# Unread products in other PSUM banks, and in more waits, of a twelve-section attention and ffn kernel

## The chip, the cores and the metric

The kernel runs on one core of a Trainium2 chip. The metric is the device time of one execution in microseconds. The median of three runs before the change is 3731.08 us (3728.47 to 3732.46).

## The reference

The state x is 16 sequences of 64 tokens with 256 features (1024 tokens in all, float32). A context of 16 x 1601 x 256 is read by four cross attentions. Twelve sections follow one another, each adding to x what it computes from a layer norm of x:

```python
x = x + L0_xattn(ln(x), ctx, ctx)     # 16 heads, softmax, a mask from tril and zero scores
x = x + L0_attn(ln(x))                # encoder of four layers with linear attention, elu(q)+1, and a relu ffn
x = x + L0_ffn(ln(x))                 # 8 experts with a capacity
x = x + L1_xattn(ln(x), ctx)          # slots: three rounds, a GRU cell
x = x + L1_attn(ln(x))                # softmax attention, 16 heads within a sequence of 64
x = x + L1_ffn(ln(x))                 # 8 small experts, two rounds
x = x + L2_xattn(ln(x), ctx, mask)    # relu squared in place of softmax
x = x + L2_attn(ln(x))                # linear attention over 64 random features per head
x = x + L2_ffn(ln(x))                 # 16 experts and a shared one
x = x + L3_xattn(ln(x), ctx)          # softmax over 1601 keys
x = x + L3_attn(ln(x))                # softmax attention with a position bias and a causal mask
x = x + L3_ffn(ln(x))                 # rows rounded to int8, an integer product
```

Each of these is written out here as a name and a note; the change touches no arithmetic of any of them.

## The kernel before, in words

The 1024 tokens are eight tiles of 128 (a tile holds two sequences), and the 256 features are two chunks of 128. The sections run in the order of `STAGES`; each opens its own pools of SBUF and PSUM tiles and closes them at its end. PSUM has eight banks of 128 x 512 float32, and each section shares them out by tags: `mm` with two or three banks for short products, `acc` for accumulators, and others. A tile of a tag has as many banks as `bufs` says. A new tile of a tag waits until the bank's last tile has been read for the last time.

Tile (the framework) plans the order of instructions from a model of their durations. Where `self.pinned` is true, the tensor engine's products (`mm`, line 2617) and transposes (`tr`, line 2630) are kept in the order in which the program calls them. The plain helpers `transpose` (line 174) and `lin_t` (line 195) call the engine themselves and are never pinned. Every engine works through its own queue in order, and an instruction that waits holds up what is behind it.

**Unread products.** `awake(pool, n, tag, bufs)` (line 2623) takes one PSUM tile of the named tag and has the tensor engine multiply the identity with 512 columns of constants into it, n times. Nobody reads the result. Each such product shows as two matmul records. In the profile they are the tile `awake`. Before the change they are called at these places that the change touches:

- `attend` in `l0_attn` (line 686) is a generator, run in turn with `project` of the other half of the tokens. For layer 0's first half (`early`) two products stand in front of `turn(s, 0)`.
- `l2_attn`: the loop at its end calls two in front of the last `project` (line 2116), in a bank of `mm`.
- `Then.turn` (line 2388), the start of the last ffn for a tile: seven, four and three for tiles 0, 6 and 7, in `mm`.
- `token_attention` (line 2652) is the body of L1 and of L3 attention; `own_input` is true for L1. Its inner `linear` normalises and transposes half of the tokens, then makes queries, keys and values; `scores(t)` and `values(t, e)` follow tile by tile, and `project(t)` two tiles later. In `values`, two groups of four transposes go to banks of `mm`, ScalarE copies them to `eT`, and `acc` (one buffer of two banks) takes the products with the values; VectorE's `rec` and then `hT` (lines 2775 and 2776) read `acc`. Unread products stand in front of the transposes (line 2755) and in front of `acc` (line 2761), and for L3 in front of the first `lin_t` (line 2699), all in `mm` with two banks.

Two more sections come into it. `l0_xattn` computes maxima of the scores per block (`maxima`, line 288), eight products per block into the four banks of the tag `w`, ahead of its main stream; `stream` (line 2504) pins the order from its step -1 on, so the first maxima are not pinned. `l2_xattn` normalises all tiles, transposes them and makes the queries through `acc` (two banks); `bk` (two banks) first serves the stream's projections of the context.

Of the kernel before, what the change touches and what calls it, by code (L numbers as in the profile page):

```python
# [12 lines left out]
F32 = mybir.dt.float32  # L13
# [7 lines left out]
P = 128  # L21
B, S, D = 16, 64, 256
T = B * S
NT = T // P
# [40 lines left out]
class Sections:  # L65
# [157 lines left out]
    def l0_xattn(self):  # L223
# [6 lines left out]
        with ExitStack() as ctx:  # L230
# [57 lines left out]
            def maxima(x, g, i):  # L288


                pm = quad()
                for r in range(4):
                    o = slice(32 * r, 32 * r + 32)
                    self.mm(
                        pm[:, r, :], x.qb[o, g].rearrange("p h s -> p (h s)"), x.kT[i][o, g, :512], start=True, stop=True)
                if i == 0:
                    nc.vector.scalar_tensor_tensor(x.z[:, g], pm[:, :, :S], 0.0, tril, ALU.is_equal, ALU.mult)
                    nc.vector.scalar_tensor_tensor(pm[:, :, :S], x.z[:, g], NEVER, pm[:, :, :S], ALU.mult, ALU.add)
                nc.vector.tensor_reduce(x.m4[:, g, :, i], pm, AX.X, ALU.max)  # L299
# [181 lines left out]
    def l0_attn(self):  # L481
# [25 lines left out]
        with ExitStack() as ctx:  # L507
# [178 lines left out]
            def attend(s, w, early=False):  # L686

                kvs = {}

                def sums(t):  # L690

                    pk = ps_kv.tile([P, 2, 512], F32, tag="kv", name="pk")
                    for g in range(2):
                        for j in range(2):
                            o = slice(j * S, (j + 1) * S)
                            self.mm(
                                pk[:, j, g * 136 : (g + 1) * 136], s.kz[o, t, g * P : (g + 1) * P], s.va[o, t, g, :],
                                start=True, stop=True)
                    kv = sb2.tile([P, 2, 2, 136], F32, tag="kv", name="kv")
                    for j in range(2):  # L700
                        V.tensor_tensor(
                            kv[:, j], pk[:, j, :272].rearrange("p (g x) -> p g x", g=2),
                            mask.unsqueeze(1).to_broadcast([P, 2, 136]), ALU.mult)
                    kvs[t] = kv

                def apply(t):
                    po = ps.tile([P, 2, 136], F32, tag="po", name="po", padded_shape=[P, 2, 256])
                    kv = kvs.pop(t)
                    for g in range(2):
                        for j in range(2):  # L710
                            self.mm(
                                po[j * S : (j + 1) * S, g, :], s.qT[:, g, t * P + j * S : t * P + (j + 1) * S],
                                kv[:, j, g, :], start=True, stop=True)
                    r = sb2.tile([P, 2, 8], F32, tag="r", name="r")
                    V.tensor_scalar(r, po[:, :, 128:136], 1e-6, None, ALU.add)
                    V.reciprocal(r, r)
                    V.tensor_tensor(
                        s.n[:, t, :].rearrange("p (g h e) -> p g h e", g=2, e=16),
                        po[:, :, 0:128].rearrange("p g (h e) -> p g h e", e=16),
                        r.unsqueeze(3).to_broadcast([P, 2, 8, 16]), ALU.mult)  # L720

                for t in range(HT):
                    sums(t)
                    yield
                    if t:
                        apply(t - 1)
                        yield
                apply(HT - 1)
                self.awake(ps, 2 if early else 0, "mm", 3)
                turn(s, 0)  # L730
                yield
                turn(s, 1)
                yield
                for t in range(HT):
                    pm = by_token(w.wo, t, s.hT)
                    V.tensor_tensor(s.y[:, t, :], pm, s.y[:, t, :], ALU.add)
                    if t % 2:
                        measure(s, s.y, t // 2)
                    yield
                    if t % 2:  # L740
                        norm(s, s.y, t // 2)
                        yield
# [1134 lines left out]
    def l2_xattn(self):  # L1877
        nc, tc, d = self.nc, self.tc, self.d
        with ExitStack() as ctx:
# [9 lines left out]
            qT = sb.tile([P, KC, T], F32, tag="qT", name="qT")  # L1889
            for t in range(NT):  # L1890
                self.normed(t, xln[:, t, :])
            self.transpose(ps, xln, xT, tag="acc")
            self.lin_t(ps, wq, xT, lambda n, h, pm: nc.vector.tensor_scalar(
                qT[:, n, h * 512 : (h + 1) * 512], pm, 0.25, None, ALU.mult), tag="acc")
            hT = xT
            own = self.c("own2")
            ones = self.c("ones")[:, :32]
# [49 lines left out]
    def l2_attn(self):  # L1947
        nc, tc, d = self.nc, self.tc, self.d
        F, HT = 64, NT // 2
        with ExitStack() as ctx:  # L1950
# [152 lines left out]
            for t in range(NT + 2):  # L2103
                if t < NT:
                    self.awake(ps, 0 if t else 2, "mm", 2)
                    kp = key_features(t)
                if 0 < t <= NT:
                    apply(t - 1, kvs.pop(t - 1))
                for _ in range((3, 3, 2, 2)[t] if t < 4 else 0):
                    next(rest)  # L2110
                if t == 3:
                    next(rest, None)
                if t < NT:
                    kvs[t] = sums(t, kp)
                if t > 1:
                    self.awake(ps, 2 if t > NT else 0, "mm", 2)
                    project(t - 2)
            self.pinned = False

# [218 lines left out]
    def l3_ffn(self, sb, sb2, ps):  # L2338
# [14 lines left out]
        class Then:  # L2353
# [32 lines left out]
                    xs[t] = sc[:, j : j + 1]  # L2386

            def turn(s, t):
                self.awake(ps, {0: 7, 6: 4, 7: 3}.get(t, 0), "mm", 2)
                pt = ps.tile([P, KC, P], BF16, tag="mm", name="trb", bufs=2, padded_shape=[P, KC, 512])  # L2390
                for c in range(KC):
                    self.tr(pt[:, c, :], xq[t][:, c * P : (c + 1) * P], identb)
                xq[t] = sb2.tile([P, KC, P], BF16, tag="f_qT", name="f_qT")
                nc.scalar.copy(xq[t], pt)
# [228 lines left out]
    def awake(self, pool, n, tag, bufs=None):  # L2623

        if n:
            pm = pool.tile([P, 512], F32, tag=tag, name="awake", **({"bufs": bufs} if bufs else {}))
            for _ in range(n):
                self.mm(pm, self.ident, self.cst[:, :512], start=True, stop=True)

# [22 lines left out]
    def token_attention(self, sb, sb2, ps, w, wo, bias_t, rows, scale, own_input, bias=None, then=None):  # L2652
# [21 lines left out]
        def linear(i):  # L2674
# [21 lines left out]
            nc.gpsimd.tensor_tensor(x, x, bo.unsqueeze(1).to_broadcast([P, HT, D]), ALU.add)  # L2696
            for n in range(4):
                if n == i == 0:
                    self.awake(ps, 0 if own_input else 3, "mm", 2)
                pm = ps.tile([P, 512], F32, tag="mm", name="lin_t", bufs=2)  # L2700
                for k in range(KC):
                    self.mm(pm, w[:, k, n * P : (n + 1) * P], xT[:, k, :], start=(k == 0), stop=(k == KC - 1))
# [48 lines left out]
        def values(t, e):  # L2751


            eT = sb2.tile([P, KC, 4, P], F32, tag="eT", name="eT")
            self.awake(ps, ({1: 2, 2: 1} if own_input else {2: 1}).get(t, 0), "mm", 2)
            for g in range(KC):
                pt = ps.tile([P, 4, P], F32, tag="mm", name="turn", bufs=2)
                for r in range(4):
                    self.tr(pt[:, r, :], e[:, r, 2 * g : 2 * g + 2, :].rearrange("p j s -> p (j s)"), self.ident)
                nc.scalar.copy(eT[:, g], pt)  # L2760
            self.awake(ps, 0 if own_input else {1: 1, 2: 1, 5: 2}.get(t, 0), "mm", 2)
            acc = ps.tile([P, 2, 512], F32, tag="acc", name="acc", bufs=1)
            at = acc[:, :, :256].rearrange("p j (k g s) -> p j k g s", k=2, g=2)
            for k in range(2):
# [12 lines left out]
                hT[:, :, t * P : (t + 1) * P].rearrange("p g (j s) -> p j g s", j=2), at[:, :, 0], rec, ALU.mult)  # L2777

        def project(t):
            pm = ps.tile([P, D], F32, tag="mm", name="lin", bufs=2, padded_shape=[P, 512])  # L2780
            for k in range(KC):
                self.mm(pm, hT[:, k, t * P : (t + 1) * P], wo[:, k, :], start=(k == 0), stop=(k == KC - 1))
# [217 lines left out]
```

## Time and profile before

| | us |
|---|---|
| median of three runs | 3731.08 |
| lowest, highest | 3728.47, 3732.46 |
| the profiled execution | 3730.16 |
| its span, first to last instruction | 3728.4 |
| TensorE matmuls busy | 3499.4 (94%) |
| VectorE, ScalarE, GpSimd busy | 1970.9, 1461.2, 1286.4 |
| mean granted TensorE clock | 0.979 |
| unread products in the profile | 104 with the constants, 5 at the start |

The profile's span is one execution; 1.8 us lie around it. The row PEclk of the page gives, in forty equal slices, the TensorE clock that was granted, in tenths. A timeline line gives the start, the length, the engine, the line of the program, the tile written and those read, and, in brackets, how long the engine had stood idle and which instruction ended that. L2619 and L2631 are the helpers `mm` and `tr`, so tile names tell the products apart. L59 is the helper that pins VectorE, ScalarE and GpSimd in `l0_attn`.

### The profile page before, as it was taken

The numbers are of one execution on the slowest core, as the hardware profiler recorded it, in microseconds if no ns is written. First come the engines' busy times: TensorE is split into PE (matmuls) and PEld (weight loads), VectorE is DVE, ScalarE is ACT, GpSimd is POOL, SyncE is SP. The second block draws the span as 40 slices with busy tenths as digits, with TensorE's granted clock in tenths as the row PEclk, the third lists the DMA queues.
The fourth block names the chain that finished last, engine by engine and source line by source line (L and its number), as shares of the span: only waits on it lengthen the run. The fifth ranks groups of instructions, "written<-read, shape, count | busy, mean of one in ns | idle before, by whom it ended". The sixth has DMA issues, their size and how long they took to land.

```text
span 3728.4 us, 71203 instructions
## 1 busy us (share of the span) xinstructions
PE 3499.4 (94%) x31177; PEld 2200.2 (59%) x31192; DVE 1970.9 (53%) x3645; ACT 1461.2 (39%) x2093; POOL 1286.4 (35%) x784
## 2 busy tenths in 40 slices
PE   9999999998999979999988989999999889999997
PEld 4555555564665655555555666667767655555554
DVE  5344333436555635655656555577767765333445
ACT  2333333333444413444433443466666612111123
POOL 2555555552101113433422100577777630000002
PEclk9999999999999979999999999999999989999998
DMA  4111001101333345442101001211111004111550
GB/s 146 38 38 38 28 30 38 38 8 50 101 93 97 116 133 170 147 147 85 64 26 41 1 6 41 72 57 38 57 38 38 11 2 175 36 41 33 241 214 13
DMA packets 108071, 259.77 MB, mean 70 GB/s; under 512 B 9609, under 2 KB 76172, under 8 KB 105456
## 3 DMA queue, kind: packets, MB, share of 16 engines
q1 hardware_dynamic: 99040, 223.14, 16.8%
q10 hardware_dynamic: 6912, 27.27, 2.3%
q0 software_dynamic: 1808, 4.80, 0.5%
q8 instruction: 245, 4.01, 0.4%
q14 instruction: 66, 0.54, 0.0%
HBM read 248.85 MB, written 6.33 MB: 68 GB/s over the span
## 4 chain that ended last, share of the span: by engine, by line
PE 75%; DVE 13%; ACT 7%; issue 2%; DMA 1%; POOL 0%; SPq 0%; ACTq 0%; DVEq 0%; POOLq 0%
PE sc L2619 15%; PE pk L2619 15%; PE lin L2619 6%; PE acc L2619 6%; PE lin_t L2619 5%; ACT e L358 5%; PE pu L2619 4%; PE gate L2166 3%; PE up L2166 3%; PE lin L216 3%; PE pc L1786 3%; PE prz L2619 2%; PE gelu_t L1700 2%; PE turn L2631 1%; PE pa L2619 1%
## 5 line engine op out<-in xcount | busy, mean ns | idle before, releaser
L2548 POOL TENSOR_TENSOR tot<-tot,e 128x1024 f32<-128x1024 f32 (+1 forms) x340 | 803.2, 2362 | 373.3 <-ACT e L358 251.0
L299 DVE TENSOR_REDUCE m<-sc 128x4 f32<-128x2048 f32 x96 | 220.1, 2293 | 271.3 <-PE sc L2619 270.2
L1929 DVE SCALAR_TENSOR_TENSOR e<-sc,row_L_xattn_nbias,free 128x2048 f32<-128x2048 f32 x104 | 244.3, 2349 | 115.5 <-PE sc L2619 113.1
L1931 ACT ACTIVATE e<-e 128x2048 f32<-128x2048 f32 x104 | 198.7, 1911 | 245.8 <-DVE e L1929 245.8
L358 ACT ACTIVATE e<-sc 128x2048 f32<-128x2048 f32 x104 | 195.2, 1877 | 237.3 <-PE sc L2619 235.7
L2619 PE MATMUL sc<-qb,kT 32*128 32x128 f32 x6656 | 245.0, 283 | 36.2 <-DVE m L313 12.3
L2619 PEld LDWEIGHTS sc<-qb,kT 32*128 32x128 f32 x6656 | 206.1, 187 | 80.6 <-issue 22.4
L2619 PEld LDWEIGHTS acc<-e,v 128*32 128x32 f32 x6656 | 169.7, 109 | 105.3 <-issue 96.0
L2619 PE MATMUL acc<-e,v 128*32 128x128 f32 x6656 | 225.9, 276 | 4.7 <-ACT e L1932 4.7
L2619 PE MATMUL pk<-wv,cT 128*128 128x256 f32 x832 | 209.8, 394 | 0.0
L2619 PE MATMUL pk<-cT,wk 128*128 128x512 f32 (+1 forms) x512 | 206.2, 531 | 3.6 <-DVE rows L329 3.6
L1932 ACT ACTIVATE e<-e 128x2048 f32<-128x2048 f32 x104 | 198.7, 1911 | 3.2
L2619 PE MATMUL pk<-wkv,cT 128*128 128x256 f32 x832 | 196.3, 386 | 0.0
L2619 PE MATMUL pk<-cT,wkv 128*128 128x512 f32 (+1 forms) x512 | 194.9, 522 | 0.0
L2619 PEld LDWEIGHTS pk<-wv,cT 128*128 128x128 f32 x832 | 149.5, 190 | 76.4 <-issue 58.9
L2619 PEld LDWEIGHTS pk<-wkv,cT 128*128 128x128 f32 x832 | 153.2, 190 | 28.5 <-issue 4.3
L1786 PE MATMUL pc<-ew,eh 128*128 128x256 f32 x640 | 156.1, 386 | 0.0
L2170 ACT ACTIVATE g<-gate 128x512 f32<-128x512 f32 x68 | 40.6, 597 | 293.4 <-PE gate L2166 293.4
L2619 PE MATMUL sc<-kT,qb 32*128 32x512 f32 (+2 forms) x1536 | 138.9, 461 | 13.8 <-DVE m L299 2.3
L1319 POOL TENSOR_TENSOR e<-e,mx 128x512 f32<-128x512 f32 x96 | 81.9, 885 | 194.3 <-DVE mx L1318 194.3
L2619 PE MATMUL pu<-cn,e 128*64 128x257 f32 (+1 forms) x1248 | 141.6, 381 | 3.3 <-DMA cn<-in_ctx_n 1.8
L2171 DVE TENSOR_TENSOR hT<-up,g 128x512 f32<-128x512 f32 x68 | 47.0, 691 | 183.2 <-PE up L2166 183.2
(544 smaller groups left out, 6425.2 us busy)
## 6 DMA issues: line engine op xcount, KB each, us to landing
cT<-in_ctx_t SPq DMA_DIRECT2D x128, 832.0 KB, 6.4
cn<-in_ctx_n SPq DMA_DIRECT2D x32, 1664.0 KB, 11.9
piece<-in_ctx_n ACTq DMA_DIRECT2D x32, 640.0 KB, 3.9
w<-in_L_attn_W SPq DMA_DIRECT2D x8, 1024.0 KB, 7.0
piece<-in_ctx_n ACTq DMA_DIRECT2D x16, 384.0 KB, 3.7
w<-in_L_ffn_W SPq DMA_DIRECT2D x16, 256.0 KB, 3.1
down<-in_L_ffn_w_down SPq DMA_DIRECT2D x16, 256.0 KB, 2.8
gate<-in_L_ffn_w_gate SPq DMA_DIRECT2D x16, 256.0 KB, 2.7
```

The costliest lines, as they stand in the source:

```text
L216: nc.tensor.matmul(pm, xT[:, k, t * P : (t + 1) * P], w[:, k, :], start=(k == 0), stop=(k == kc - 1))
L299: nc.vector.tensor_reduce(x.m4[:, g, :, i], pm, AX.X, ALU.max)
L358: nc.scalar.activation(e, pm, AF.Exp, scale=0.25)
L1319: pin(nc.gpsimd.tensor_tensor(p.e, p.e, p.mx.unsqueeze(2).to_broadcast(p.shape), ALU.subtract))
L1700: nc.tensor.matmul(pm, w[:, c, lo : lo + m], cT[:, c, :], start=(c == 0), stop=(c == nk - 1))
L1786: nc.tensor.matmul(pc[:, n, j, :], s.eh[i][:, c, tok], ew2[:, c, cols], start=False, stop=(c == 3))
L1929: nc.vector.scalar_tensor_tensor(e16, pm16, nb, free[:, at : at + P].unsqueeze(1).to_broadcast([P, 16, P]), ALU.add, ALU.mult)
L1931: nc.scalar.activation(e, e, AF.Relu)
L1932: nc.scalar.activation(e, e, AF.Square)
L2166: nc.tensor.matmul(pm[-1], w[:, k, n * P : (n + 1) * P], xT[:, k, tok], start=(k == 0), stop=(k == KC - 1))
L2548: nc.gpsimd.tensor_tensor(tot[:w], x.first if c == 1 else tot[:w], e[:w], ALU.add)
L2619: ins = self.nc.tensor.matmul(*args, **kw)
```

## The change

Five calls move to another tag: the pair before L2 attention's last `project` goes from `mm` to `pk`; those of `Then.turn`, of `linear`, and both of `values` go from `mm` to `acc`. `awake` gets a second form of tile for these two tags, whose tiles are two banks wide; it writes the first of the two.

Six places get products that had none: two in front of the first maxima of the first cross attention (`acc`, not pinned); one in front of the first `apply` of `attend` for layer 0's first half (`mm`); two in front of the transposes at the start of `l2_xattn` (`bk`; `self.pinned` is true from there to the end of the queries, which pins these two products alone, as `transpose` and `lin_t` don't look at it); three in L1 attention's `linear` in front of the first `lin_t`; two in L3 attention's `values` for tile 1; and two in front of L1 attention's last `project` (`acc`).

In `attend`, the pair that stood in front of `turn(s, 0)` stands in front of `turn(s, 1)`.

```diff
@@ l0_xattn: maxima
                 pm = quad()
+                if x.b == g == i == 0:
+                    self.awake(ps, 2, "acc")
@@ l0_attn: attend
                     if t:
+                        self.awake(ps, 1 if early and t == 1 else 0, "mm", 3)
                         apply(t - 1)
                         yield
                 apply(HT - 1)
-                self.awake(ps, 2 if early else 0, "mm", 3)
                 turn(s, 0)
                 yield
+                self.awake(ps, 2 if early else 0, "mm", 3)
                 turn(s, 1)
@@ l2_xattn
+            self.pinned = True
+            self.awake(ps, 2, "bk")
             self.transpose(ps, xln, xT, tag="acc")
             self.lin_t(ps, wq, xT, lambda n, h, pm: nc.vector.tensor_scalar(
                 qT[:, n, h * 512 : (h + 1) * 512], pm, 0.25, None, ALU.mult), tag="acc")
+            self.pinned = False
@@ l2_attn
-                    self.awake(ps, 2 if t > NT else 0, "mm", 2)
+                    self.awake(ps, 2 if t > NT else 0, "pk", 1)
                     project(t - 2)
@@ l3_ffn: Then.turn
-                self.awake(ps, {0: 7, 6: 4, 7: 3}.get(t, 0), "mm", 2)
+                self.awake(ps, {0: 7, 6: 4, 7: 3}.get(t, 0), "acc", 1)
@@ awake
-            pm = pool.tile([P, 512], F32, tag=tag, name="awake", **({"bufs": bufs} if bufs else {}))
+            kw = {"bufs": bufs} if bufs else {}
+            if tag in ("pk", "acc") and bufs:
+                pm = pool.tile([P, 2, 512], F32, tag=tag, name="awake", **kw)[:, 0]
+            else:
+                pm = pool.tile([P, 512], F32, tag=tag, name="awake", **kw)
@@ token_attention: linear
                 if n == i == 0:
-                    self.awake(ps, 0 if own_input else 3, "mm", 2)
+                    self.awake(ps, 3, "acc", 1)
@@ token_attention: values
-            self.awake(ps, ({1: 2, 2: 1} if own_input else {2: 1}).get(t, 0), "mm", 2)
+            self.awake(ps, {1: 2, 2: 1}.get(t, 0), "acc", 1)
...
-            self.awake(ps, 0 if own_input else {1: 1, 2: 1, 5: 2}.get(t, 0), "mm", 2)
+            self.awake(ps, 0 if own_input else {1: 1, 2: 1, 5: 2}.get(t, 0), "acc", 1)
             acc = ps.tile([P, 2, 512], F32, tag="acc", name="acc", bufs=1)
@@ token_attention: project
         def project(t):
+            self.awake(ps, 2 if own_input and t == NT - 1 else 0, "acc", 1)
```

## The prediction

> **What bounds the kernel now.** First the page's busy shares, the granted clock and the chain that ended last:
>
> ```profile
> PE 3499.4 (94%) x31177; PEld 2200.2 (59%) x31192; DVE 1970.9 (53%) x3645; ACT 1461.2 (39%) x2093; POOL 1286.4 (35%) x784
> PEclk9999999999999979999999999999999989999998
> PE 75%; DVE 13%; ACT 7%; issue 2%; DMA 1%; POOL 0%; SPq 0%; ACTq 0%; DVEq 0%; POOLq 0%
> ```
>
> TensorE is the bound over most of the span, at a mean granted clock of 0.979. It stops only in the prologues and at the ends of the stages, where the chain passes to VectorE (13%) and ScalarE (7%). All edits lie there. So I read the timeline of all engines around each edit, and the stretches view for the clock. Two waits and what follows:
>
> ```profile
> 31.22:34.64 3.42, 1.15 (x6) 0.35 (x9) 2.90 (x3) 0.59 (x1) 0.00 (x0) 1.00 1.10 347
> 34.64:38.05 3.41, 3.41 (x13) 1.58 (x8) 1.81 (x1) 0.00 (x0) 0.00 (x0) 0.50 0.14 44
> 1911.95:1915.36 3.41, 1.49 (x8) 0.80 (x8) 3.41 (x10) 1.40 (x3) 1.68 (x2) 1.00 0.25 100
> 1915.36:1918.78 3.42, 1.72 (x2) 0.84 (x3) 3.38 (x5) 2.91 (x1) 3.16 (x2) 0.50 0.00 0
> ```
>
> Columns: stretch, length, busy time of PE, PEld, DVE, ACT, POOL, then granted clock. The clock changes on a grid of 3.41 us: a stretch with only 1.15 or 1.49 us of matmuls is followed by one at half clock. In this trace stretches with under some 1.4 us always are, those over 2 us hardly ever. So a wait that is filled pays twice: the product no longer stands behind it, and the next 3.41 us may run at full clock (up to 1.7 us each).
>
> **What a product costs.** The two at 61.63 us take 1.94 us: 0.97 us each at full clock. A moved product brings at most its 0.97 us; a new one brings only clock, and costs 0.97 us if its wait isn't there.
>
> **Moved products (token attention, the second linear attention, the last ffn).**
>
> ```profile
> 3606.14 1.04 PE L2631 MATMUL tr<-cst,xln 128*128 128x128 f32 x8
> 3609.99 2.84 PE L2619 MATMUL awake<-cst 128*128 128x512 f32 x6 [2.81 <-DVE xT L127]
> 3612.67 7.30 PE L2619 MATMUL lin_t<-xT,wqkv 128*128 128x512 f32 x16
> ```
>
> The three products in front of the L3 attention's lin_t want a bank that holds transposes; they wait 2.81 us for xT, which is what lin_t itself waits for. In acc they start at 3607.18 and end at 3610.0; lin_t starts at 3610.1, 2.6 us earlier. What is late next: ScalarE clears vm from 3610.21 to 3613.83, so its first qb ends at 3614.6 and the third lin_t product waits 1.0 us for that bank. Gain 1.6.
>
> ```profile
> 1947.48 1.99 PE L2619 MATMUL lin<-wqkv,xT 128*128 128x256 f32 x8
> 1951.55 2.40 PE L2619 MATMUL awake<-cst 128*128 128x512 f32 x4 [2.08 <-DVE vm L2720]
> 1953.75 1.92 PE L2631 MATMUL turn<-cst,e 128*128 128x128 f32 x8
> ```
>
> L1 attention, second tile: acc is free (hT read it until 1948.75), so the two products fill 1949.5 to 1951.4 and the turns start at 1951.55: 1.94, plus 0.7 for the half clock that falls on products and turns. Third tile: 0.93, of which 0.8 is left, as eT's copies stand behind ScalarE's exp until 1963.86.
>
> L3 attention, values. Third tile: the first product starts 1.38 us earlier, but the copies of eT wait for the exp that ends at 3657.49; the second then no longer stands between eT and acc: acc at 3658.0 for 3659.07, gain 1.0. Sixth tile: the pair starts at 3685.4 in place of 3687.67; acc starts when eT is there, 3687.7 for 3691.38. VectorE reaches rec after f_q at 3690.3 for 3693.47: 3.2, of it 1.1 at full clock, 2.1 from the half clock.
>
> ```profile
> 3086.36 1.13 PE L2619 MATMUL lin<-wo,hT 128*128 128x256 f32 x4
> 3089.22 3.47 PE L2619 MATMUL awake<-cst 128*128 128x512 f32 x4 [1.73 <-DVE x L425]
> 3092.49 1.27 PE L2619 MATMUL lin<-wo,hT 128*128 128x256 f32 x4
> ```
>
> End of L2 attention: pk's readers (kv) end at 3085.7, so the pair runs from 3087.5 to 3089.4, and the last lin starts when hT is there, 3089.6 in place of 3092.49. VectorE had waited 3.76 us for that lin, so all of it passes on: 1.55 at full clock, 1.5 from the half clock.
>
> The last ffn's 7 + 4 + 3 products: no gain. The seven wait for hT's read of acc (3668.2 for 3667.68), yet still end at 3674.6 before f_xq lets trb start at 3675.44; the four and three start without a bank wait already. Range 0 to -1.2.
>
> **First linear attention** (third bank of mm, all free). A new product before the first apply stands at 900.24, where TensorE doesn't wait, and everything to 909.06 hangs on TensorE: +1.0. The moved pair leaves the place before turn(0) for the one before turn(1); neither turn waits there, so the pair's 1.94 us only change sides of a lin: 0.
>
> **New products.**
> - First maxima (two): VectorE can't start them before 31.00 (it does the gate biases), so the 1.94 us only use up the wait of 2.27 us before 34.34: 0, and the half-clock stretch from 34.64 goes, TensorE being busy through it: -1.7. These are not pinned, the planner places them: between -1.7 and +1.9.
> - L1 attention's lin_t (three, 2.9 us): TensorE waits 2.93 us there, acc is free: 0, and lin_t takes 7.1 in place of 9.93 us: -2.8.
> - L3 attention, second tile (two): they fill the 2.08 us before 3644.18; the copy of eT still ends at 3647.48: 0, and -0.4 of clock.
> - Before the L2 cross attention (two, bk): TensorE waits 1.75 us before 2320.00. Which bank bk gets isn't seen: between 0 and +0.9 if it still holds the last ffn output, read until 2318.71. I take 0, and -1.9 of clock (second transposes 1.97 for 1.09, lin_t 8.64 for some 7.2, less the waits for copies).
> - Before the last project of L1 attention (two, acc):
>
> ```profile
> 1993.63 1.13 PE L2619 MATMUL lin<-wo,hT 128*128 128x256 f32 x4
> 1996.05 0.41 DVE L2776 TENSOR_TENSOR hT<-acc,rec 128x256 f32<-128x256 f32 x1
> 1996.60 1.10 PE L2619 MATMUL lin<-wo,hT 128*128 128x256 f32 x4 [1.84 <-DVE hT L2776]
> ```
>
> Here the bank isn't free: acc has one buffer, and hT, for which project waits, is its last reader. The products can't start before 1996.6 either: +1.94, and behind them queue project, x, and the next stage's transposes. Below that only if VectorE norms xi in the meantime, or the clock stays up after 2000.7: 0 to +1.94, I take +1.94.
>
> [...]
>
> **The sum.** At full clock: 1.0 - 1.94 - 0.8 - 1.6 - 1.0 - 1.1 - 1.55 + 1.94 = -5.05 us. Clock: -1.7 - 2.8 - 0.7 - 1.9 - 1.5 - 0.4 - 2.1 = -11.1. [...] So I keep three quarters, -8.4: -13.4 in all. The profiled execution took 3730.16 us (span 3728.4 and 1.8 around it), 0.9 below the median of the three runs; 3730.2 - 13.4 is 3716.8, set against the median 3717.7.
>
> **Rivals.**
> [...]
> - The unpinned pair and the pair before the L2 cross attention land elsewhere, so they do nothing: 0.75 x (1.7 + 1.9) = 2.7 less gain, 3720.4.
> - Slower: banks that are freed by the very read that ends the wait, as before project. Each product then pays its 0.97 us bare. The twelve new ones cost 11.6, the moved ones bring nothing: 3742.7. With only the new ones bare it would be level (11.6 - 8.0 - 0.75 x 4.3 = +0.4); it decides from there on, with each moved product that stays behind its wait. Against it are the read times of acc above, 0.8 us or more ahead in four of five places.
>
> **Chances.** Forecast (3709 to 3723.5) 0.52; below it 0.04; elsewhere-rival 0.10; direct time only 0.22; slower rival, whole or in part, 0.12. What a measurement can tell from no change is 0.2%, 7.5 us: faster means below 3723.6, which takes nearly all of the first three and little of the fourth: 0.65; slower, above 3738.5: 0.09; the rest 0.26. Range 3709 to 3731: it takes in direct time only, with the first pair bare too, and leaves out the 0.04 below and some 0.11 above.
>
> **What would show it.** Right: awake right after the transposes at the L3 prologue, lin_t 2.5 us sooner; no half clock after the first maxima or in L1's lin_t; acc in the sixth tile right behind eT. Wrong: awake with a wait for hT or for rec in the values; half clock at those places all the same, or as many such stretches as before. Before L1's last project I expect awake with a wait for hT, and project 1.9 us after it.

## The result, and the profile after

| | before | after |
|---|---|---|
| median, us | 3730.9 (10 runs) | 3722.8 (10 runs) |
| lowest to highest, us | 3726.5 to 3736.3 | 3715.5 to 3725.8 |
| profiled execution, us (span) | 3730.16 (3728.4) | 3722.76 (3721.0) |
| mean granted clock of the profiled execution | 0.979 | 0.981 |
| unread products with the constants | 104 | 116 |

The ratio of the times is 0.9977, with a 95% interval of 0.9969 to 0.9986: 8.1 us less, between 5.2 and 11.6. That is inside the predicted range and 5.1 us above the forecast of 3717.7. The two profiles differ by 7.4 us.

The page of the kernel after, the busy shares, the granted clock in 40 slices and the chain that ended last:

```profile
PE 3504.1 (94%) x31201; PEld 2202.4 (59%) x31216; DVE 1972.7 (53%) x3645; ACT 1460.8 (39%) x2093; POOL 1286.2 (35%) x784
PEclk9999999999999979999999999999999989999999
PE 75%; DVE 13%; ACT 8%; issue 3%; DMA 1%; POOL 0%; SPq 0%; ACTq 0%; DVEq 0%; POOLq 0%
```

Nothing of this page tells the two kernels apart: the slices of the clock are too coarse, and TensorE is even 4.7 us busier. The places have to be looked at one by one.

**The first maxima** (timeline of TensorE after; start, length, engine, line, tiles, and the wait ahead in brackets; L2625 is the helper `mm`, L2641 is `tr`):

```profile
25.44 2.31 PE L2625 MATMUL pk<-cT,wk 128*128 128x512 f32 x5
27.58 1.88 PE L2625 MATMUL awake<-cst 128*128 128x512 f32 x4
29.39 1.14 PE L2625 MATMUL sc<-kT,qb 32*128 32x512 f32 x8
30.46 3.70 PE L2625 MATMUL pk<-cT,wk 128*128 128x512 f32 x8
36.44 1.14 PE L2625 MATMUL sc<-kT,qb 32*128 32x512 f32 x8 [2.28 <-DVE m L301]
```

Before, the same place ran like this, behind the first group of maxima:

```profile
26.65 5.42 PE L2619 MATMUL pk<-cT,wk 128*128 128x512 f32 x12
34.34 1.85 PE L2619 MATMUL sc<-kT,qb 32*128 32x512 f32 x8 [2.27 <-DVE m L299]
```

The pair stands where the program calls it, in front of the first group of maxima. There TensorE had waited for nothing. The wait of 2.27 us was in front of the second group, and it is still there, at 2.28. Before, twelve matmul records of projections lay between the two groups; now there are eight, and the other four come behind the wait: the planner changed their order. The stretches of the clock after (length, busy time of PE, PEld, DVE, ACT and POOL, then the granted clock) show that half clock stays too:

```profile
34.10:37.52 3.42, 1.14 (x10) 0.35 (x9) 2.19 (x1) 0.58 (x1) 0.00 (x0) 1.00 0.33 106
37.52:40.93 3.41, 3.41 (x8) 1.49 (x5) 2.29 (x1) 0.00 (x0) 0.00 (x0) 0.50 0.02 5
```

**L1 attention's lin_t** (stretches after): the thin stretch of 1.49 us is gone, and with it the half clock.

```profile
1914.82:1918.24 3.42, 2.47 (x12) 1.19 (x11) 2.80 (x10) 0.55 (x2) 1.63 (x5) 1.00 0.54 198
1918.24:1921.65 3.41, 3.05 (x8) 1.13 (x7) 3.37 (x4) 3.41 (x2) 3.33 (x2) 1.00 0.00 0
```

**The moved products and L1's last project** (timeline of TensorE after: second tile of L1, last project of L1, end of L2 attention, L3's prologue, sixth tile of L3):

```profile
1948.65 1.99 PE L2625 MATMUL lin<-wqkv,xT 128*128 128x256 f32 x8
1950.48 1.88 PE L2625 MATMUL awake<-cst 128*128 128x512 f32 x4
1952.73 1.06 PE L2641 MATMUL turn<-cst,e 128*128 128x128 f32 x8 [0.37 <-DVE vm L2730]
...
1992.18 1.13 PE L2625 MATMUL lin<-wo,hT 128*128 128x256 f32 x4
1995.16 1.95 PE L2625 MATMUL awake<-cst 128*128 128x512 f32 x4 [1.84 <-DVE hT L2786]
1996.95 1.03 PE L2625 MATMUL lin<-wo,hT 128*128 128x256 f32 x4
...
3087.07 2.08 PE L2625 MATMUL lin<-wo,hT 128*128 128x256 f32 x4
3088.94 1.93 PE L2625 MATMUL awake<-cst 128*128 128x512 f32 x4
3090.70 1.03 PE L2625 MATMUL lin<-wo,hT 128*128 128x256 f32 x4
...
3608.27 2.84 PE L2625 MATMUL awake<-cst 128*128 128x512 f32 x6 [1.55 <-DVE x L427]
3610.95 7.30 PE L2625 MATMUL lin_t<-xT,wqkv 128*128 128x512 f32 x16
...
3681.62 1.88 PE L2625 MATMUL awake<-cst 128*128 128x512 f32 x4
3684.05 0.94 PE L2625 MATMUL acc<-eT,vm 64*32 64x64 f32 x64 [0.55 <-ACT eT L2770]
```

In the second tile, at the end of L2 attention and in the sixth tile, awake starts straight behind the product ahead of it, with no wait for a bank. Before L1's last project it waits for hT (the releaser in brackets), and project comes 1.8 us after it, as the forecast had it. At L3's prologue awake does not start at once: it waits for VectorE's x of the section before, which runs from 3607.80 to 3608.21, and so it starts 1.55 us late, and lin_t behind it 1.5 us after the last xT is there (3609.47).

**Place by place.** To see what each place is worth I matched TensorE's instructions of both traces and took how much longer or shorter the stretch from one instruction to another is after than before. The change of the kernel's span is the sum of such differences. "Clock" is a part of it: half of the time that TensorE was busy in stretches at half clock, unread products not counted (half, as the four lin matmuls of a project in L2 attention take 2.07 us after in such a stretch, at 3041.82, and 1.13 at full clock, at 3053.55). It counts in full even where the slower clock only shortens a wait that follows.

| place | forecast, us | after less before, us | of it clock |
|---|---|---|---|
| first maxima (new pair) | -1.7 | +1.75 | 0 |
| first linear attention (new product) | +1.0 | +0.21 | -0.5 |
| L1 lin_t (new three) | -2.8 | -2.55 | -2.6 |
| L1 values, second and third tile (moved) | -3.44 | -2.69 | -1.3 |
| before L1's last project (new pair) | +1.94 | +1.72 | 0 |
| before L2 cross attention (new pair) | -1.9 | -1.12 | -1.0 |
| end of L2 attention (moved) | -3.05 | -2.74 | +0.7 |
| L3 prologue (moved) | -1.6 | -1.25 | 0 |
| L3 values, second, third, sixth tile | -4.6 | -6.17 | -4.0 |
| last ffn (moved) | 0 | +0.49 | 0 |
| sum of the places | -16.15 | -12.35 | -8.7 |
| everywhere else | +2.75 (the quarter of the clock taken off) | +5.0 | +6.6 |

The places with an edit gave 12.35 us; elsewhere 5.0 us were lost in this pair of profiles, where nothing was edited. The largest losses are 2.4 us in the first lin_t (half clock from 13.62 us), 1.7 in the L1 ffn (half clock from 2293.72), 1.9 in L2 attention up to its last but one project (half clock from 3082.20) and 1.6 in the L2 ffn's gate (half clock from 3095.86, next to the end of L2 attention); smaller gains stand against them. Of the 1.12 us at the L2 cross attention, 0.3 lie in the L1 ffn ahead of the pair.

Taken together, clock and all else come out very differently from the forecast: the clock gave 2.1 us (-8.7 at the places, +6.6 elsewhere) where the forecast had 8.4, and the rest gave 5.3 where it had 5.05. The time at half clock fell only from 159.6 to 142.5 us.

### The profile page after: what moved, and what is told of

Its sections match the earlier page's. It is cut to its first block, busy times and chain, and to the rows that moved or that the text cites. A ratio compares the mean times of both kernels' runs of the same rounds, so it can differ in the third digit from the quotient of the medians.

```text
span 3721.0 us, 71257 instructions
## 1 busy us (share of the span) xinstructions
PE 3504.1 (94%) x31201; PEld 2202.4 (59%) x31216; DVE 1972.7 (53%) x3645; ACT 1460.8 (39%) x2093; POOL 1286.2 (35%) x784
## 4 chain that ended last, share of the span: by engine, by line
PE 75%; DVE 13%; ACT 8%; issue 3%; DMA 1%; POOL 0%; SPq 0%; ACTq 0%; DVEq 0%; POOLq 0%
PE sc L2625 15%; PE pk L2625 15%; PE lin L2625 6%; PE acc L2625 6%; PE lin_t L2625 5%; ACT e L360 5%; PE pu L2625 4%; PE gate L2172 3%; PE up L2172 3%; PE lin L216 3%; PE pc L1789 3%; PE prz L2625 2%; PE gelu_t L1703 2%; PE turn L2641 1%; PE pa L2625 1%
## 5 line engine op out<-in xcount | busy, mean ns | idle before, releaser
L2625 PE MATMUL sc<-qb,kT 32*128 32x128 f32 x6656 | 245.0, 283 | 36.3 <-DVE m L315 12.4
L2625 PEld LDWEIGHTS sc<-qb,kT 32*128 32x128 f32 x6656 | 206.1, 187 | 80.7 <-issue 22.4
L2625 PEld LDWEIGHTS acc<-e,v 128*32 128x32 f32 x6656 | 170.0, 110 | 105.4 <-issue 96.0
L2625 PE MATMUL acc<-e,v 128*32 128x128 f32 x6656 | 226.3, 276 | 4.7 <-ACT e L1938 4.7
L2625 PE MATMUL pk<-cT,wk 128*128 128x512 f32 (+1 forms) x512 | 208.1, 535 | 3.6 <-DVE rows L331 3.6
L2625 PE MATMUL pk<-wv,cT 128*128 128x256 f32 x832 | 208.6, 393 | 0.0
L2625 PE MATMUL pk<-wkv,cT 128*128 128x256 f32 x832 | 196.3, 386 | 0.0
L2625 PE MATMUL pk<-cT,wkv 128*128 128x512 f32 (+1 forms) x512 | 194.9, 522 | 0.0
L2625 PEld LDWEIGHTS pk<-wv,cT 128*128 128x128 f32 x832 | 149.3, 190 | 75.8 <-issue 57.7
L2625 PEld LDWEIGHTS pk<-wkv,cT 128*128 128x128 f32 x832 | 153.2, 190 | 28.5 <-issue 4.3
L2625 PE MATMUL sc<-kT,qb 32*128 32x512 f32 (+2 forms) x1536 | 138.8, 459 | 13.8 <-DVE m L301 2.3
L2625 PE MATMUL pu<-cn,e 128*64 128x257 f32 (+1 forms) x1248 | 141.7, 381 | 1.5 <-POOL e L1332 1.5
```

Of the source, the lines that this page charges most:

```text
L2625: ins = self.nc.tensor.matmul(*args, **kw)
```

## The experiments

Theories. **A**: the moves bring all of the gain; of the new places some gain as forecast, and two or three pay for themselves (placed where nothing waits, or behind their own bank). **B**: only direct time counts, as the clock comes and goes. **C**: the banks are not what matters. All times were compared with the kernel before on the same chip, so that ratios can be set side by side. In timelines the helpers mm and tr stand at L2619 to L2629 and L2631 to L2645, by the kernel.

### Only the moves, and only the new places

Against the changed kernel, the first leaves out all six new places (two of them shown):

```diff
-                if x.b == g == i == 0:
-                    self.awake(ps, 2, "acc")
...
-            self.awake(ps, 2 if own_input and t == NT - 1 else 0, "acc", 1)
...
```

The second undoes all moves (two of them shown):

```diff
-                    self.awake(ps, 2 if t > NT else 0, "pk", 1)
+                    self.awake(ps, 2 if t > NT else 0, "mm", 2)
...
-                self.awake(ps, {0: 7, 6: 4, 7: 3}.get(t, 0), "acc", 1)
+                self.awake(ps, {0: 7, 6: 4, 7: 3}.get(t, 0), "mm", 2)
...
```

> The kernel before with only the moves: the five changes of tag and the pair that changes sides of a turn in the first linear attention; none of the six new places. Theory (both profiles, place by place): the moved products gave about 2.7 us in L1's values, 1.4 at the L3 prologue, 5.5 in L3's values and 3.2 at the end of L2 attention, of which 1.5 came back in the next prologue: 11 us less than before, about 3720, ratio 0.997. So the moves would be more than the whole gain of the change. Rival (only direct time counts, half-clock stretches reappear elsewhere): 8.0 us less, 3723. Rival (the banks make no difference): within 2 us of before. In the profile awake at the end of L2 attention starts without a wait for x, and the sixth tile's acc comes about 3.5 us sooner.

> The changed kernel with the moved products put back into their old banks and place; only the six new places are left. Theory (offsets of the two profiles): first maxima +1.9, first apply +0.2 to +1, L1 lin_t -2.1, L2 cross attention -0.7, L3 second tile 0, L1's last project +1.8: between +1 and +2, about 3732, no gain at all. The forecast's terms would give -1.7 +1.0 -2.8 -1.9 -0.4 +1.94 = -3.9, about 3727. Rival (only direct time counts): +2.9, 3734.

| | ratio to before (95%) | median, us | before on this chip |
|---|---|---|---|
| moves only | 0.9972 (0.9961 to 0.9984) | 3721.2 | 3731.4 |
| new places only | 1.0003 (0.9997 to 1.0010) | 3731.5 | 3731.4 |

The moves alone bring 10 us, all that the change brings, and the new places bring nothing. C is out. A and B can't be told apart by these times: 6 to 15 us less includes the 8.0 of B as well as the 11 of A, and -1 to +4 us includes the +2.9 of B as well as A's +1 to +2. In the profile of "moves only" the clock part, counted as above, is even 2.2 us worse than before (156.8 us at half clock for 159.6), so that its 8.3 us are all of the other kind. Nor did anything of the end of L2 attention come back there in the next section, as had been expected. The new places did not fail for want of clock: over the runs the mean granted clock rose from 0.9785 to 0.9817, just as in the changed kernel. What they won there they paid for with direct time. In the profile of "new places only": first maxima +1.76, first linear attention +0.49, last project +2.02, against L1's lin_t -2.55 and the L2 cross attention -1.08. The two gaining places gain by clock alone (-2.6 and -1.0), so B, for which the clock is worth nothing, is wrong at these places.

### Without three of the new places

```diff
-                    self.awake(ps, 2, "acc")
+                    self.awake(ps, 0, "acc")
...
-                        self.awake(ps, 1 if early and t == 1 else 0, "mm", 3)
+                        self.awake(ps, 0, "mm", 3)
...
-            self.awake(ps, 2 if own_input and t == NT - 1 else 0, "acc", 1)
+            self.awake(ps, 0, "acc", 1)
```

> The changed kernel without three of its new places: the pair in front of the first maxima, the product in front of the first apply, and the pair in front of L1's last project. Theory: these cost 1.9, about 0.2 (up to 1.0) and 1.8 us, so the kernel is 3.9 us faster than with them, about 3719. The forecast's own terms would give -(-1.7 +1.0 +1.94) = -1.2, about 3721.6. If the first pair only moved time around within the grid of the clock, -2 us. In the profile the pair's absence puts the first maxima ahead of the gate biases on VectorE again, and project starts right behind hT.

Ratio to before 0.9959 (0.9942 to 0.9975), median 3716.2. The step from 0.9977 is 6.7 us, but the two intervals overlap; the time alone does not prove it. The places do: against the changed kernel the maxima are 1.76 us shorter, the first linear attention 0.40 and the last project 1.62, in all 3.8. The forecast's terms (1.2 us) are out, by the first pair. One expectation failed: VectorE does its gate biases ahead of the first maxima here as well, as it did before the change.

### The last project's pair in another bank

```diff
-            self.awake(ps, 2 if own_input and t == NT - 1 else 0, "acc", 1)
+            self.awake(ps, 2 if own_input and t == NT - 1 else 0, "mm", 2)
```

> The changed kernel with one edit: the pair in front of L1 attention's last project goes to a bank of mm (two) in place of acc. Theory (hT's read of acc is what the pair waits for): in mm it starts right after the project before it and fills the wait of 1.84 us, and the last project comes straight behind hT, about 1.8 us sooner; 3721. Rival (the bank is not what holds the pair): no difference in where it starts, project 1.8 us behind hT as in the changed kernel. The row of awake at that place tells them apart: with a wait for hT, or without; the time itself, 1.8 us of 3723, is hardly more than what five rounds can tell.

Timeline of TensorE at this place in this kernel:

```profile
1994.96 1.13 PE L2625 MATMUL lin<-wo,hT 128*128 128x256 f32 x4
1995.93 1.88 PE L2625 MATMUL awake<-cst 128*128 128x512 f32 x4
1997.84 1.13 PE L2625 MATMUL lin<-wo,hT 128*128 128x256 f32 x4
```

The wait for hT in front of awake is gone. From one lin to the next it is 2.88 us here and 4.77 in the changed kernel: 1.9 us, the bare price of the pair. The bank was the cause of the wait, as forecast. Ratio to before 0.9958 (0.9944 to 0.9972), median 3715.2; most of its distance to the changed kernel is more than this place can give, and it isn't shown where it comes from: its profiled execution took 3724.3, the highest of its five runs.

### Without the small groups

```diff
     def awake(self, pool, n, tag, bufs=None):
-        if n:
+        if n > 3:
```

> The changed kernel with all unread products left out where they stand in groups of one to three: 65 products in 33 places go, the groups of four and more stay. The waits that open are shorter than 3.4 us. Theory (waits of 1.7 to 2.9 us make thin stretches of 3.41 us, and these are followed by half clock): the mean granted clock falls from 0.982 to about 0.970, and the kernel is slower by 33 places x some 0.7 us, less the 4 us of the products that stand bare: +19, within +10 to +35; 3742. [...]

```profile
PE 3478.1 (93%) x31086; PEld 2203.8 (59%) x31086; DVE 1967.1 (53%) x3645; ACT 1461.0 (39%) x2093; POOL 1285.7 (35%) x784
PEclk9999999998999979999998999999999989999998
```

Busy shares and clock on the page of this kernel: three of the forty slices of PEclk are lower than in the changed kernel (the tenth, around the end of the first linear attention; the twenty-second, from L1 attention into the L1 ffn; and the last). The mean clock fell from 0.982 to 0.970, to the digit what I expected, and stretches at half clock grew from 142.5 to 222.5 us in the profiles. It is not long stops that made the difference: in this profile TensorE stops for longer than a stretch of 3.41 us six times, in the changed kernel five times, and yet 80 us more were at half clock. What goes with half clock here is how full a stretch of 3.41 us is. Over the twelve profiles, all 108 stretches at full clock that held under 1.4 us of matmuls were followed by half clock, 88 of 222 with 1.4 to 2.0 us, and 25 of some 12,100 with more; in those of before and after alone it is 19 of 19, 16 of 41 and 4 of 2032.

But the time is not what I expected. The ratio to before is 0.9991 (0.9982 to 1.0000), so the kernel is about 5 us slower than the changed one and not 19. The accounting of the two profiles says where the error is: clock +33.1 us, a full 1.0 us for each of the 33 places, where I had 0.7; but the rest is -28.5 us, where I had put 4. Counted so, the 65 products, at 0.97 us each, cost 0.44 us each on average. That is an upper figure, and so is the 33: where half clock only shortens the wait behind it, the time counts as lost by the clock and again as won by the rest. What the runs show is the difference: unread products in 33 short waits raise the clock a good deal and bring about 5 us, with intervals that just overlap.

### The good places together

```diff
-                    self.awake(ps, 2, "acc")
+                    self.awake(ps, 0, "acc")
...
-                        self.awake(ps, 1 if early and t == 1 else 0, "mm", 3)
+                        self.awake(ps, 0, "mm", 3)
...
-            self.awake(ps, 2 if own_input and t == NT - 1 else 0, "acc", 1)
+            self.awake(ps, 2 if own_input and t == NT - 1 else 0, "mm", 2)
```

> The changed kernel without the pair at the first maxima and without the product in front of the first apply, and with the pair in front of L1's last project in a bank of mm: the two earlier experiments put together. Theory (place by place): -1.75 for the maxima, -0.2 to -0.8 for the apply, -1.7 for the project, so 3.7 to 4.3 us less than the changed kernel: 3718.5, and between 0 and 2 us less than without that pair, by the clock behind project alone. Rival (the earlier gains were runs with luckier stretches of the clock): within 2 us of the changed kernel, 3722.

Ratio 0.9961 (0.9947 to 0.9975), median 3714.3 beside 3728.4 for before. The same as without the pair (0.9959): in its own bank it costs nothing, and what it brings can't be told from nothing.

### The first pair where the wait is

```diff
-                if x.b == g == i == 0:
+                if x.b == g == 0 and i == 1:
                     self.awake(ps, 2, "acc")
...
-            self.pinned = k >= -1
+            self.pinned = k >= -1 or (extra is not None and -8 <= k <= -7)
...
-                for bj, j in jobs[h : h + 1] if h == 0 else jobs[1:]:
+                now = jobs[h : h + 1] if h == 0 else jobs[1:]
+                if extra is not None and k == -7:
+                    now = jobs if h else []
+                for bj, j in now:
```

These edits go on top of the kernel of the section above. The first calls the pair for the second group of maxima; the other two write down the order of these few products, so that the planner can't move the pair.

> As the kernel before this one in the list, and a pair at the first maxima again, this time in front of the second group of maxima, where the wait is, with the order of these few products written down (six projections' halves, maxima, six, the pair, maxima). Theory: here the pair fills the wait of 2.27 us, costs nothing at full clock, and the half clock behind it goes: maxima and projections from 34 to 40 us are 1.7 us shorter than without the pair. Rival (a product in the prologue always costs its 1.9 us, wherever it stands): +1.9. In the profile: awake begins with no wait for a maximum, the second maxima begin when VectorE is done, and the next 3.41 us are at full clock.

The second group of maxima without the pair (the kernel of the section above, where the same twelve records of projections stand ahead of it), then timeline of TensorE and stretches of the clock with it:

```profile
36.44 1.79 PE L2625 MATMUL sc<-kT,qb 32*128 32x512 f32 x8 [2.27 <-DVE m L301]
```

```profile
26.78 1.14 PE L2628 MATMUL sc<-kT,qb 32*128 32x512 f32 x8
27.85 5.42 PE L2628 MATMUL pk<-cT,wk 128*128 128x512 f32 x12
33.11 1.88 PE L2628 MATMUL awake<-cst 128*128 128x512 f32 x4
35.55 1.14 PE L2628 MATMUL sc<-kT,qb 32*128 32x512 f32 x8 [0.56 <-DVE m L301]
```

```profile
32.52:35.93 3.41, 2.85 (x10) 1.10 (x12) 2.81 (x3) 0.58 (x1) 0.00 (x0) 1.00 0.85 270
35.93:39.35 3.42, 3.42 (x24) 2.34 (x16) 2.29 (x1) 0.65 (x2) 0.00 (x0) 1.00 0.02 5
```

The wait of 2.27 us is 0.56, the stretch holds 2.85 us of matmuls in place of 1.14, and the next one is at full clock. The place is 1.64 us shorter than without the pair, all of it clock, and 3.40 shorter than in the changed kernel. The forecast's -1.7 was right for a pair in the wait, and wrong for where this change puts it. Ratio 0.9953 (0.9941 to 0.9965), median 3711.8.

### A pair more at the start of the L2 ffn

```diff
             self.transpose(ps, xln, xT)
+            self.awake(ps, 2, "up")
             sc = sb.tile([P, NT, E], F32, tag="sc", name="sc")
```

This goes on top of the kernel of the section above.

> As the kernel before this one in the list, and a pair more at the start of the L2 ffn, in the free bank of up, where the changed kernel's profile shows a stretch with 1.6 us of matmuls in 3.41 and half clock in the next one or two (1.7 us lost in gate). The planner puts one of the two in front of the first transposes and one between them. Theory (a thin stretch lowers the clock of the next): gate stays at full clock, -1.7, less up to 0.7 for the product between the transposes: about -1. Rival (half clock is handed on to the next prologue anyway): 0 to +1. The profile's stretches from 3080 to 3100 tell, rather than the time.

Stretches of the clock there, first without this pair (the kernel of the section above), then with it:

```profile
3084.03:3087.45 3.42, 1.61 (x9) 0.94 (x9) 3.42 (x14) 0.21 (x2) 0.00 (x0) 1.00 0.84 297
3087.45:3090.86 3.41, 3.41 (x17) 3.41 (x17) 1.08 (x3) 1.61 (x4) 0.00 (x0) 0.50 1.01 416
3090.86:3094.27 3.41, 3.41 (x5) 1.36 (x5) 0.00 (x0) 1.22 (x4) 0.00 (x0) 0.50 1.06 445
```

```profile
3084.99:3088.41 3.42, 2.49 (x13) 1.36 (x12) 3.42 (x14) 0.32 (x2) 0.00 (x0) 1.00 0.92 314
3088.41:3091.82 3.41, 3.41 (x21) 2.45 (x22) 0.97 (x3) 2.45 (x6) 0.00 (x0) 1.00 1.03 422
3091.82:3095.23 3.41, 3.41 (x15) 2.04 (x14) 0.54 (x1) 3.36 (x5) 0.00 (x0) 1.00 1.04 437
```

1.61 us of matmuls in a stretch: half clock for two stretches. 2.49 us: none. The place (3086 to 3110 us of before) is 3.3 us shorter, more than the 1 us expected. So what the end of L2 attention had given back in the next section of the changed kernel can be had: the thin stretch after it was there to be filled. Ratio to before 0.9949 (0.9936 to 0.9962), median 3709.9 beside 3728.4: 19 us less than before. Its interval lies below that of the changed kernel, so this version beats both. It overlaps that of the kernel without this last pair, so the time alone does not show what the pair is worth.

### Unread products where nothing waits

Against the kernel of the section above:

```diff
-                self.awake(ps, {0: 7, 6: 4, 7: 3}.get(t, 0), "acc", 1)
+                self.awake(ps, {0: 7, 6: 4}.get(t, 0), "acc", 1)
```

and, in the second of the two kernels, this too:

```diff
-                    self.awake(ps, 2 * g, "mm", 2)
+                    self.awake(ps, 0 if i else 2 * g, "mm", 2)
```

> The last kernel (all three places mended, a pair more at the start of the L2 ffn) without the three unread products in front of the last tile's turn in the last ffn. Theory (a product costs its 0.97 us where nothing else is waited for): f_xq of the last tile is there at 3707.02, but trb starts at 3709.45, behind the three; without them trb starts at 3707.1 and the end is 2.4 us earlier; no clock is lost, since only transposes and one product of 0.39 us come after. 3707.5. Rival (the forecast's reading that these start without a wait for a bank and so cost and gain nothing): no change, 3710.

> As the kernel before this one in the list, without the pair between the two pqp of the second half in L2 attention. Theory: it stands at 3041.12 between two products that wait for no other engine, in a stretch at full clock, so the 1.94 us come off what follows, up to VectorE's kp at 3054, which the next wait hangs on: between 0 and -1.9, as kp waits for its own work. Rival (ScalarE's read of pqp is the next wait there, so the pair only fills it): 0, with half clock in the next stretch, up to +1.7.

The last two turns of the last ffn (trb are their transposes, f_lin their products), first with the three products, then without:

```profile
3705.91 0.28 PE L2645 MATMUL trb<-identb,f_xq 128*128 128x128 bf16 x2
3706.65 0.39 PE L2629 MATMUL f_lin<-wb,f_qT 128*128 128x256 bf16 x2 [0.47 <-ACT f_qT L2401]
3706.88 2.74 PE L2629 MATMUL awake<-cst 128*128 128x512 f32 x6
3709.45 0.28 PE L2645 MATMUL trb<-identb,f_xq 128*128 128x128 bf16 x2
```

```profile
3709.28 0.28 PE L2645 MATMUL trb<-identb,f_xq 128*128 128x128 bf16 x2
3710.02 0.39 PE L2629 MATMUL f_lin<-wb,f_qT 128*128 128x256 bf16 x2 [0.47 <-ACT f_qT L2401]
3710.43 0.28 PE L2645 MATMUL trb<-identb,f_xq 128*128 128x128 bf16 x2
```

From one trb to the other it is 1.15 us and was 3.54: 2.4 us, as expected (0.7 of it is lost again in this profile, as the four products ahead ran partly at half clock, 4.60 us for 3.93). The three stood bare. The forecast had looked only at whether they wait for a bank, and not at whether anything else is waited for at that place. In L2 attention the rival is right:

```profile
3048.57 1.71 PE L2629 MATMUL pqp<-qn,proj 32*128 32x512 f32 x8
3052.29 1.26 PE L2629 MATMUL pqp<-qn,proj 32*128 32x512 f32 x8 [2.01 <-ACT qp L2046]
```

Without the pair, the second pqp waits 2.01 us for ScalarE's read of the first; the pair only fills that. The half clock that this rival expected behind the open wait is there too: pk and lin behind the second pqp take 3.63 and 2.07 us (from 3053.48 and 3057.03), where they take 1.98 and 1.13 with the pair (from 3044.26 and 3046.17 in the kernel of the section above).

The times do not bear the 2.4 us out: 0.9960 (0.9946 to 0.9974) without the three, 0.9948 (0.9934 to 0.9961) without the pair too, and 0.9949 with both, so the three kernels can't be told apart. The profiles of both show a stop in L1's cross attention that none of the other kernels' has: ScalarE begins scs late, and TensorE waits 4.40 and 3.72 us for it there. No edit is near. What ScalarE waits for at that place isn't seen, and it stays open whether it belongs to these two kernels or to their runs.

## Why the prediction came out as it did

**The total.** The sign and the range were right. The forecast of -13.4 us was 5.3 too much. The places gave -12.35 for -16.15 at full value, and elsewhere 5.0 were lost for the 2.75 that I had taken off (a quarter of 11.1 leaves 8.3, where the sum says 8.4). By kind, the direct time is right in sum (5.3 for 5.05), in part by luck, as the first pair's loss is in it and gains stand against that; of the clock's 8.4 only 2.1 remain in this pair of profiles.

**First maxima: the step that failed.** The prediction has "so the 1.94 us only use up the wait of 2.27 us before 34.34: 0, and the half-clock stretch from 34.64 goes". The pair is called in front of the first group; the wait is in front of the second, with projections between them. I had seen that the planner places this pair, and gave its range as -1.7 to +1.9, but took the end at which it moves to the wait. It went to the other: +1.75. That is 3.4 of the 3.8 us that the places fell short. With the pair in the wait the term is -1.64, so the mechanism holds and the place was wrong.

**The clock terms at the places.** -2.55 for -2.8 in L1's lin_t, all of it clock. The L2 cross attention gave 1.1 for 1.9: bk was free, so that the pair cost nothing, but a second wait of 1.52 us between the transposes left one of the two half-clock stretches. In L3's values the sixth tile gave 5.1 us (between 3676 and 3694 of before) where I had 3.2, and the third 1.65 where I had 1.0; the second lost 0.6 where I had a gain of 0.4, as its pair pays part of its own time (clock -1.1, the rest +1.7).

The sixth tile's number is mostly luck. Its row before, in "new places only", where the pair is still in mm, and the first acc without the small groups, where there is no pair:

```profile
3687.67 3.78 PE L2619 MATMUL awake<-cst 128*128 128x512 f32 x4 [2.27 <-ACT eT L2760]
3687.25 1.98 PE L2625 MATMUL awake<-cst 128*128 128x512 f32 x4 [2.27 <-ACT eT L2771]
3690.53 0.94 PE L2625 MATMUL acc<-eT,vm 64*32 64x64 f32 x64 [2.27 <-ACT eT L2770]
```

The same wait of 2.27 us is open in all three, but only the profile of before is at half clock behind it. With the pair unmoved the place is 3.4 us shorter than before, and without any pair 5.1 us, as much as with the pair moved. So the move is worth some 1.7 us here, for 1.1 at full clock in the forecast, and the half clock that it was to remove goes away without it too.

How firm the other places are, the profiles of the experiments that leave them as in the change can tell (counted in the same way, to 0.3 us): the first maxima +1.75 to +1.76, L1's lin_t -2.5 to -2.6, the last project +1.7 to +2.0, the end of L2 attention -2.6 to -3.1 and L3's prologue -1.25 come again each time; L1's values lie between -1.7 and -3.5, the L2 cross attention between -0.3 and -1.1, and the second and third tile of L3 between -1.8 and +2.0.

**Direct terms.** Before L1's last project: +1.72 for +1.94, and for the reason given. The end of L2 attention: -2.74 for -3.05. L3's prologue: -1.25 for -1.6; "in acc they start at 3607.18" was wrong, since awake waits there for x, which ends at 3608.2. In the first linear attention the product cost 0.73 and not 1.0, and 0.5 came back by the clock.

**The quarter taken off.** It stood for half clock that moves to other places; no run shows a quarter. In the seven profiles whose kernels have edits at these places alone, what happens outside them differs from before by +5.0, +5.4, -4.6, -0.4, +6.6, +1.8 and +1.8 us (in the order of the sections above, the changed kernel first). That is nearly as large as the change itself, and it is no share of the gain: "new places only" won 4.6 us there. One profile could not give this term; it belonged in the range, and not in the forecast's sum.

**The rivals.** "Elsewhere" was right for the maxima and wrong for bk. "Direct time only" (the -5.05, and nothing by the clock) is nearest to how this pair of profiles divides, and the times of the first two experiments allow it. It falls by the places where only the clock changed: L1's lin_t, the pair in the wait of the first maxima (1.64 us) and the L2 ffn (3.3 us). "Slower" held at one place, L1's last project. That the new places bring nothing in sum was not among my cases; I had them at -3.9 (-1.7 + 1.0 - 2.8 - 0.4 - 1.9 + 1.94).

## What to carry to other kernels

What an unread product was worth here depended on how full its 3.41 us stretch was without it (1.14 us of matmuls without the pair at the first maxima, and half clock behind it; 2.85 with it, and full clock): fill the wait itself, in a bank whose last reader is done before the wait begins (before L1's last project the pair waited 1.84 us in acc, and not at all in mm), and see in the timeline that no other engine is held up behind it. Where a planner places it, look up the wait in its order, not in the program's; between two groups of products there may be others that it will move. Each one that stands where nothing is waited for costs its full time (0.97 us here), so that a set of them can raise the clock and not the speed (0.9785 to 0.9817 at a ratio of 1.0003 with the new places alone). And one profile before and one after can't say what the clock gave at a place: look whether the half clock is still there in another run that leaves the place alone.

## What was not expected of the hardware

- The spread of one kernel's runs goes with the granted clock. Over some 140 runs of these kernels and of before, 0.001 of mean clock goes with about 2.4 us within a kernel, and what is left scatters by 1.9 us, where the runs of one kernel scatter by 2 to 6. Between kernels the mean clock says little: the new places raised it from 0.9785 to 0.9817 and won nothing, and without the small groups it is 0.970 at a time not above that of before.
- The grid of the clock lay differently to the start of the span in each of these profiles: half-clock stretches begin at 34.64 us before, 37.52 after and 36.80 with the good places together, and a stretch begins at 35.93 with the first pair where the wait is, which leave 0.51, 3.39, 2.67 and 1.80 us when ten stretches of 3.413 us are taken off.
